# A graph-attention layer: the order of a group's work in the main loop is turned

## The chip, the cores and the metric

The kernel runs on one core of one Trainium2 chip. The metric is the device time of one execution in microseconds (us), the median of several runs. Five engines work side by side, each through its own queue in order: TensorE (PE), VectorE (DVE), ScalarE (ACT), GpSimd (POOL) and SyncE (SP). An instruction that waits holds up what is queued behind it on its engine.

## The reference

The layer has 12,500 nodes with 128 features and 212,500 edges, 12,500 of them self loops, sorted by target node (`dst`). There are 8 heads of 16 features.

```
Q, K, V = x @ WQ, x @ WK, x @ WV            # (N, 8, 16) each
Eh      = edge_attr @ WE                     # (E, 8, 16)
score   = exp(clip((K[src] * Q[dst] / sqrt(16) * Eh).sum(-1), -5, 5))
msg     = V[src] * score
wV, Z   = segment_sum(msg, dst), segment_sum(score, dst)
h       = x + wV / (Z + 1e-6)
h       = (h - mean) * rsqrt(var + 1e-5) * gamma + beta    # over the nodes
out     = layernorm(x + h)                   # over the features
```

## The kernel before

The edges are cut into 1,661 tiles of 128. A window of 64 nodes has its edges in four tiles, and a group is two windows, so eight tiles; there are 208 groups. `hx` keeps x in on-chip memory, features by nodes, and takes the sums in place.

The kernel has three stages. First the table: K and V of all nodes go to a table `kvd` in HBM, one row of 256 floats a node (up to about 105 us). Then the main loop, one group an iteration, to about 2,710 us. Then the two norms and the output.

The steps of a group g, with their lines and engines, are these. A line number is that of the kernel before.

- `gather` (L205, POOL): eight indirect transfers, each fetching 128 rows of K|V by source node into a slot. There are eight slots, and a ninth later. The loop hands queued transfers to POOL in two lots of four (`issue`); the first transfer of a lot waits (`pace`) for a step on DVE, the first lot for the message of the previous group (`SENT[g - 1]`), the second for the second half of the products (`PARTS[g][1]`).
- `load`, `load_rel`, `load_quad` (SP): edge features of two groups in one transfer of 1 MB, and the edges' places inside their window, on all partitions (`rb`, or `rbq` for four groups).
- `q_window` (L471, ACT) copies the x of the two windows to `xw`; `q_mm` (L502, PE) and `q_out` (L506, ACT) make Q of the 128 nodes in `qs`.
- `eh_mm` (L515, PE) and `eh_out` (L522, ACT): edge features times WE, into `wt`. `turned_onehot` (L492, DVE) compares places with node numbers, giving nodes by edges (`ot`). `qe_mm` (L529, PE) multiplies Q with it, so that each edge gets Q of its target.
- `both_halves` (L539, DVE) multiplies the two; `turn_back` (L547, PE) transposes the product, edge by edge, to `ps_t`.
- `products` (L562, DVE) multiply the gathered K by it, `scores` (L569, DVE) sum over each head, `clip_exp` clips on DVE (L578) and takes exp on ACT twice (L579, L580). `message` (L584, DVE) multiplies V by it and frees the slot.
- `onehot` (L482, L484, L485, DVE): edges by nodes (`oh`, two buffers). `gather_sum` (L599, L600, PE) multiplies it with the messages, which sums them by node in the PSUM bank `ps_a`; `sums_out` (L605, ACT) copies the sums out.
- `denom` (L609), `recip` (L612), `attn` (L616, all DVE) divide; `add_x` (L625, L626, PE) transposes the result and adds x; `x_out` (L630, ACT) writes it to `hx`. Batch-norm statistics (L633, DVE) follow where enough nodes are done.

No planner is at work: each engine takes its instructions in the order in which the loop's body (from L761) writes them, with waits added by the framework where a tile is read, or a buffer is used again. `sum_ps` (`ps_a`) holds three things side by side in one bank: the sums, Q's product and add_x's result. `ps_e`, `ps_q`, `ps_t` have two banks each. The loop before writes in iteration g, per engine:

- DVE: products(g), denom(g−2), scores(g), clip(g), recip(g−2), turned_onehot(g+2), both_halves(g+1), attn(g−2), message(g), onehot(g+1)
- PE: add_x(g−3), q_mm(g+2), gather_sum(g−1), eh_mm(g+2), turn_back(g+1), qe_mm(g+2)
- ACT: exps(g), x_out(g−3), q_out(g+2), sums_out(g−1), eh_out(g+2), q_window(g+3)

Of the kernel before, what the change touches and what calls it, by code (L numbers as in the profile page):

```python
# [8 lines left out]
F32 = mybir.dt.float32  # L9
BF16 = mybir.dt.bfloat16  # L10
U8 = mybir.dt.uint8
# [49 lines left out]
def gnn_kernel(  # L61
# [42 lines left out]
    kvd = dram.tile([N, 2 * P], F32, name="kvd")  # L104
    full = usizes.count(U) // 2
    assert usizes[:2 * full] == [U] * (2 * full)
    relT = dram.tile([2, full * U, P], BF16, name="relT")
    rel_end = dram.tile([T - full * G, P], BF16, name="rel_end")

# [99 lines left out]
    def issue(n=0):  # L211
        while len(queued) > n:
            f, *a = queued.pop(0)
            f(*a)
# [66 lines left out]
    def within(f, g):  # L281
        return f(g) if 0 <= g < NG else None
# [33 lines left out]
    def place(r):  # L316
        nc.vector.tensor_copy(vw(rel, r), vw(rel_i, r))
        nc.vector.tensor_tensor(vw(rel, r), vw(rel, r), bc(base_f, r), op=OP.subtract)
        end = ustarts[r[0]] + (r[1] - r[0]) * r[2]
        for t in range(ustarts[r[0]], end, P):  # L320
            n = min(P, end - t)
            ps, of = spare_ps, rel[:, t:t + n]
            apart = t + n <= full * G
            assert (t % G == n % G == 0) if apart else t >= full * G
            if apart:
                turned_of = wp.tile([P, P], F32, name="relby", bufs=1)
                nc.vector.tensor_copy(turned_of[:, :n].rearrange("p (h w j) -> p h w j", h=2, j=U),
                                      of.rearrange("p (w h j) -> p h w j", h=2, j=U))
                of = turned_of[:, :n]
            nc.tensor.transpose(ps[:n], of, ident)  # L330
            row = wp.tile([P, P], BF16, name="relrow", bufs=2)
            nc.vector.tensor_copy(row[:n], ps[:n])
            if apart:
                for h in (0, 1):
                    nc.scalar.dma_start(relT[h, t // 2:(t + n) // 2, :], row[h * n // 2:(h + 1) * n // 2])
            else:
                nc.scalar.dma_start(rel_end[t - full * G:t - full * G + n, :], row[:n])
# [4 lines left out]
        return bass.AP(tensor=relT.tensor, offset=relT.offset + (h * full + g) * U * P, ap=[[0, WN], [1, n * U * P]])  # L342

    def load_quad(q):
        t = late[0].tile([P, RQ, U * P], BF16, name="rbq", bufs=2)
        for h in (0, 1):
            nc.sync.dma_start(t[h * WN:(h + 1) * WN].rearrange("p a b -> p (a b)"), places(h, RQ * q, RQ))
        for k in range(RQ):
            RB[RQ * q + k] = t[:, k, :]
# [3 lines left out]
    def load_rel(g):  # L353
        if g // RQ in quads:
            return
        RB[g] = wp.tile([P, U * P], BF16, name="rb", bufs=2)
        for h in (0, 1):
            t, n = ustarts[2 * g + h] - full * G, usizes[2 * g + h]
            nc.sync.dma_start(RB[g][h * WN:(h + 1) * WN, :n * P], places(h, g, 1) if g < full else bass.AP(
                tensor=rel_end.tensor, offset=rel_end.offset + t * P, ap=[[0, WN], [1, n * P]]))  # L360
# [77 lines left out]
    def nt(g):  # L438
        return sizes[g]
# [15 lines left out]
    def project_main(g):  # L455
        half = [table_tile(2 * (g % 2) + a) for a in (0, 1)]
        KV[g] = lambda a, b, c, n=P: half[a // 4][:, a % 4:a % 4 + b - a, c:c + n]
        for a in (0, 4):
            project(g, a, lambda: turned().rearrange("p (a b) d -> p a (b d)", b=2), True)

    def q_window(g):
        if g not in BASE:
            n = 2 if g % 2 == 0 and g + 1 < NG else 1
            _, at = nc.values_load_multi_w_load_instructions(
                base_i[0:1, 2 * g:2 * (g + n)], engines=(ET.Activation,), min_val=0, max_val=N,
                skip_runtime_bounds_check_because="node ids")
            for k in range(n):
                BASE[g + k] = at[2 * k:2 * k + 2]
        XW[g] = wp.tile([P, P], F32, name="xw", bufs=6)
        for h in (0, 1):  # L470
            nc.scalar.activation(XW[g][:, h * WN:(h + 1) * WN], hx[:, ds(BASE[g][h], WN)], AF.Copy)  # L471

# [29 lines left out]
        return nc.tensor.matmul(PQ[g], XW[g], w_q, start=True, stop=True)  # L502

    def q_out(g):
        QS[g] = wp.tile([P, P], F32, name="qs", bufs=1)
        nc.scalar.activation(QS[g], PQ[g], AF.Copy, scale=0.25)  # L506

    EH = {}
# [22 lines left out]
    def ehqe(g):  # L531
        eh_mm(g)
        eh_out(g)
        qe_mm(g)
# [6 lines left out]
    def turn_back(g):  # L541

        PW[g] = []
        for h, (a, b) in enumerate(halves(g)):
            ps = turned()
            for j in range(b - a):
                nc.tensor.transpose(ps[:, j, :], WT[g][h][:, j * P:(j + 1) * P], ident)  # L547
            PW[g].append(ps)
# [15 lines left out]

    def scores(g, h=None):
        if not h:
            SS[g] = wp.tile([P, G, H], F32, name="s", bufs=1)
        for a, b in ranges(g, h):
            step = nc.vector.tensor_reduce(SS[g][:, a:b, :], KV[g](a, b, 0).rearrange("p t (h d) -> p t h d", d=DH),  # L569
                                           axis=AX.X, op=OP.add)  # L570
        PARTS.setdefault(g, []).append(step)

    def clip_exp(g, h=None):
        a, b = (0, nt(g)) if h is None else halves(g)[h]
        if not h:
            MSG[g] = wp.tile([P, G, W], F32, name="msg", bufs=2)
        s = SS[g][:, a:b, :]
        nc.vector.tensor_scalar(s, s, 5.0, -5.0, op0=OP.min, op1=OP.max)  # L578
        nc.scalar.activation(exp_ps(g)[:, a:b, :], s, AF.Exp)  # L579
        nc.scalar.activation(MSG[g][:, a:b, P:], s, AF.Exp)  # L580

    def message(g, h=None):
        for a, b in ranges(g, h):
# [91 lines left out]
    def both_halves(g):  # L675
        both(g, 0)
        both(g, 1)
# [4 lines left out]
             [(turned_onehot, 1)]]  # L682
    first_step = NQ - len(steps) - 5
    assert first_step > 3 and max(piece) < first_step + 14
    windows = {first_step + 2: (0, 1), first_step + 8: (2,)}
    for q in range(NQ):
        for w in windows.get(q, ()):
            q_window(w)
# [19 lines left out]
    load_kv()  # L708
    load(1)
    load_rel(2)  # L710
    ehqe(0)
    q_mm(1)
    q_out(1)
    both_halves(0)
    turn_back(0)
    ehqe(1)
    onehot(0)


    done = set()  # L720
# [31 lines left out]
    def within_checks(g):  # L752
        if g >= first_check and (g - first_check) % every == 0:
            check((g - first_check) // every)
# [6 lines left out]
    for g in range(NG - 2):  # L761
        if g % 2 == 0:
            load(g // 2 + 2)
        within(load_rel, g + 3)
        if (g + 6) % RQ == 0 and (g + 6) // RQ in quads:
            load_quad((g + 6) // RQ)
        within(products, g)
        within(denom, g - 2)
        within(scores, g)
        within(clip_exp, g)  # L770
        within(recip, g - 2)
        within(turned_onehot, g + 2)
        within(both_halves, g + 1)
        late_x = g + 1 < nxg and g + 1 not in SLOT
        if late_x:
            turn_x(g + 1, 0, True)
            turn_x(g + 1, 4, True)
        within(add_x, g - 3)
        within(q_mm, g + 2)
        if g < LATE + 4:  # L780
            issue()
        else:
            left = len(queued)
            for k, step in enumerate([SENT[g - 1], PARTS[g][1]]):
                if len(queued) == left - k * G // 2:
                    pace(step)
                issue(max(0, left - (k + 1) * G // 2))
        within(gather_sum, g - 1)
        if not late_x:
            within(eh_mm, g + 2)  # L790
        within(x_out, g - 3)
        within(q_out, g + 2)
        within(sums_out, g - 1)
        if late_x:
            project_main(g + 1)
            within(eh_mm, g + 2)
        within(eh_out, g + 2)
        within(q_window, g + 3)
        within(turn_back, g + 1)
        within(qe_mm, g + 2)  # L800
        within(attn, g - 2)
        within(message, g)
        within(onehot, g + 1)
        if g == 2:
            load_last()
        for r in runs[1:]:
            if g == max(4, r[0] // 2 - 12):
                place(r)
        within_checks(g)
        while free and todo and not pending:  # L810
            load_x()
        bn_parts(2 * g - 5, 2 * g - 3)
        if g == NG - 5:
            assert done >= set(range(NPRE))
            norm_first()
        if g == LATE - 1:
            tps.close()
            late.append(tps.enter_context(tc.tile_pool(name="late", bufs=1)))
        if g == LATE - 2:
            free.append(NSLOT)  # L820
            load_kv()
    last = NG - 1
    g = last - 1
    within_checks(g)
    within_checks(last)
    flag = [nc.values_load(bad_i[0:1, 0:1], min_val=0, max_val=1 << 20,
# [330 lines left out]
```

## Time and profile before

| what | value |
|---|---|
| median of 3 runs | 2780.78 us (2774.32 to 2784.37) |
| profiled execution | 2785.63 us, its span 2783.5 us |
| mean granted TensorE clock | 0.823 |
| busy share | PE 66%, DVE 56%, POOL 58%, ACT 21% |
| bytes moved | 386.26 MB, 139 GB/s |

The span runs from the first instruction to the last of the profiled execution. Busy is the time in which an engine executes; waits are idle time, put down to what ended last by the profile. A row of the groups reads: line, engine, operation, output and inputs, count, then busy us and mean ns of one, then the idle time just before and what ended most of it. A row of the timeline reads: start in us, duration in us, queue or engine, line, operation, count, and in brackets the idle time before it. The ends of matmuls are modelled.

### The profile page before, as it was taken

How to read it: one execution, taken by the hardware profiler on the slowest of the kernel's cores; microseconds unless marked ns; L12 is line 12 of the kernel's file. 1: busy time of each engine (PE TensorE's matmuls, PEld its weight loads, DVE VectorE, ACT ScalarE, POOL GpSimd, SP SyncE). 2: the span in 40 equal slices, each digit the busy share in tenths (PEclk: the TensorE clock that was granted, in tenths of full speed). 3: DMA queues.
4: the chain of work that ended last, by engine and by line, in shares of the span. 5: the costliest groups of instructions: out<-in, count | busy, mean ns of one | idle time of the engine just before them, and what ended most of it. 6: DMA issues, size and time to landing. Idle time of an engine off the chain costs nothing. (4 is left out here: it accounts for less than half of the span.)

```text
span 2783.5 us, 29268 instructions
## 1 busy us (share of the span) xinstructions
PE 1823.7 (66%) x8998; PEld 1169.4 (42%) x8998; DVE 1551.7 (56%) x3152; ACT 586.4 (21%) x2272; POOL 1602.5 (58%) x1697
## 2 busy tenths in 40 slices
PE   6667765766656756656566666666665666665688
PEld 5444443444333434433334334444343344333456
DVE  2335555555565646655555555655555565555578
ACT  1122121122111212221112121221211122211125
POOL 5644655655556656556565656556565665565524
PEclk8878878888888878887887878878787888788899
DMA  6634434444444444444444434444444444444443
GB/s 220 229 119 125 142 117 144 140 140 137 122 142 124 135 146 138 142 130 127 139 128 129 151 123 132 142 134 145 126 130 138 129 134 142 134 125 140 133 165 113
DMA packets 122250, 386.26 MB, mean 139 GB/s; under 512 B 34205, under 2 KB 42950, under 8 KB 108134
## 3 DMA queue, kind: packets, MB, share of 16 engines
q0 software_dynamic: 78704, 213.62, 26.2%
q1 hardware_dynamic: 40196, 169.36, 17.8%
q10 hardware_dynamic: 3186, 1.34, 0.2%
q8 instruction: 73, 1.20, 0.2%
q14 instruction: 91, 0.75, 0.1%
HBM read 364.56 MB, written 19.63 MB: 138 GB/s over the span
## 5 line engine op out<-in xcount | busy, mean ns | idle before, releaser
L205 POOL DMA_INDIRECT slot<-kvd,srcs x1597 | 1513.1, 947 | 1064.5 <-DVE rz L609 532.0
L529 PE MATMUL ps_q<-ot,qs 64*128 64x512 f32 x832 | 303.0, 812 | 722.1 <-ACT qs L506 709.0
L600 PE MATMUL ps_a<-msg,oh 128*128 128x136 f32 (+1 forms) x3322 | 557.2, 309 | 5.6 <-issue 4.7
L482 DVE TENSOR_TENSOR oh<-ps_m,rel_i 128x512 f32<-128x512 f32 x208 | 142.5, 685 | 698.6 <-remote 662.7
L600 PEld LDWEIGHTS ps_a<-msg,oh 128*128 128x128 f32 (+1 forms) x3322 | 457.9, 182 | 87.5 <-issue 64.0
L562 DVE TENSOR_TENSOR slot<-slot,ps_t 128x512 f32<-128x512 f32 x410 | 267.5, 679 | 336.7 <-remote 166.2
L515 PE MATMUL ps_e<-ea,w_e 128*128 128x512 f32 x832 | 399.4, 601 | 10.3 <-issue 7.0
L529 PEld LDWEIGHTS ps_q<-ot,qs 64*128 64x128 f32 x832 | 77.5, 228 | 768.6 <-ACT qs L506 728.1
L547 PE MATMUL ps_t<-ident,wt 128*128 128x128 f32 x1661 | 246.0, 284 | 138.2 <-DVE wt L539 71.8
L630 ACT ACTIVATE hx<-ps_a 128x64 f32 x408 | 90.6, 222 | 1070.4 <-remote 842.4
L547 PEld LDWEIGHTS ps_t<-ident,wt 128*128 128x128 f32 x1661 | 192.8, 143 | 289.2 <-DVE wt L539 140.4
L539 DVE TENSOR_TENSOR wt<-wt,ps_q 128x512 f32<-128x512 f32 x416 | 264.6, 673 | 20.6 <-remote 13.4
L522 ACT ACTIVATE wt<-ps_e 128x512 f32<-128x512 f32 x416 | 237.3, 612 | 61.8 <-PE ps_t L547 27.5
L569 DVE TENSOR_REDUCE s<-slot 128x64 f32<-128x1024 f32 (+1 forms) x208 | 249.9, 1202 | 0.2
L584 DVE TENSOR_TENSOR msg<-slot,ps_m 128x1024 f32<-128x1024 f32 (+2 forms) x209 | 247.5, 1186 | 0.4 <-ACT ps_m L579 0.3
L579 ACT ACTIVATE ps_m<-s 128x64 f32<-128x64 f32 (+1 forms) x209 | 47.5, 227 | 922.8 <-DVE s L578 554.5
L515 PEld LDWEIGHTS ps_e<-ea,w_e 128*128 128x128 f32 x832 | 144.9, 192 | 116.4 <-issue 111.2
L625 PEld LDWEIGHTS ps_a<-ident,at 128*128 128x128 f32 x408 | 74.6, 229 | 200.0 <-ACT xw L471 98.4
L625 PE MATMUL ps_a<-ident,at 128*128 128x128 f32 x408 | 120.0, 383 | 2.5 <-issue 1.1
L502 PE MATMUL ps_a<-w_q,xw 128*128 128x128 f32 x416 | 98.0, 324 | 8.2 <-ACT xw L471 4.6
L626 PE MATMUL ps_a<-xw,ident 128*128 128x128 f32 x408 | 95.5, 323 | 0.0
L471 ACT ACTIVATE xw<-hx 128x64 f32 x416 | 86.6, 271 | 12.1 <-DMA relT<-relrow 8.3
(174 smaller groups left out, 1406.3 us busy)
## 6 DMA issues: line engine op xcount, KB each, us to landing
ea<-eaT SPq DMA_DIRECT2D x103, 1024.0 KB
slot<-kvd,srcs POOLq DMA_INDIRECT x1597
rbq<-relT SPq DMA_DIRECT2D x94, 256.0 KB
kvd<-slot SPq DMA_DIRECT2D x12, 512.0 KB
kvd<-t SPq DMA_DIRECT2D x12, 512.0 KB
slot<-xT SPq DMA_DIRECT2D x6, 1024.0 KB
out<-o SPq DMA_DIRECT2D x23, 256.0 KB
hx<-xT SPq DMA_DIRECT2D x11, 512.0 KB
```

The source lines that it names most:

```text
L205: return nc.gpsimd.indirect_dma_start(out=out, out_offset=None, in_=table, in_offset=bass.IndirectOffsetOnAxis(ap=srcs[:, e:e + 1], axis=0))
L482: nc.vector.tensor_tensor(one, iota_ps[:, None, :].to_broadcast([P, n, P]), r[:, :n, None].to_broadcast([P, n, P]), op=OP.is_equal)
L515: nc.tensor.matmul(eh, w_e, EA[g][:, a:b, :].rearrange("p a b -> p (a b)"), start=True, stop=True)
L522: nc.scalar.activation(t[:, :(b - a) * P], EH[g][h], AF.Copy)
L529: nc.tensor.matmul(QE[g][h], QS[g][r], OT[g][r, :(b - a) * P], start=True, stop=True)
L539: nc.vector.tensor_tensor(t, t, QE[g][h], op=OP.mult)
L547: nc.tensor.transpose(ps[:, j, :], WT[g][h][:, j * P:(j + 1) * P], ident)
L562: step = nc.vector.tensor_tensor(kv, kv, PW[g][i][:, :b - a, :], op=OP.mult)
L569: step = nc.vector.tensor_reduce(SS[g][:, a:b, :], KV[g](a, b, 0).rearrange("p t (h d) -> p t h d", d=DH), axis=AX.X, op=OP.add)
L584: step = nc.vector.tensor_tensor(MSG[g][:, a:b, :P].rearrange("p t (h d) -> p t h d", d=DH), KV[g](a, b, P).rearrange("p t (h d) -> p t h ...
L600: nc.tensor.matmul(AGG[g][WN if j >= n else 0:], OH[g][j], MSG[g][:, j, :], start=(j == 0), stop=(j == n - 1))
L625: nc.tensor.matmul(ps, AT[g], ident, start=True, stop=False)
```

## The change

The order of the loop's body is turned. In iteration g the engines now have:

- DVE: message(g−1), both_halves(g+1), products(g), scores(g), clip(g), turned_onehot(g+3), onehot(g), denom, recip and attn of g−2
- PE: eh_mm(g+2), turn_back(g+1), qe_mm(g+2), add_x(g−3), q_mm(g+3), gather_sum(g−1)
- ACT: sums_out(g−2), eh_out(g+2), q_window(g+4), x_out(g−3), q_out(g+3), exps(g)

So the message of a group is written in the next iteration, its one-hot in the same iteration as its scores, and its sums are copied out one iteration after they are made; Q is made a group sooner. `clip_exp` is split, so that the clip and the exps can be placed apart. The edges' places are kept as bytes (U8) in place of BF16, which halves the tiles and the transfers of them; `xw` has 8 buffers for 6, `qs` and `s` 2 for 1. The gathers are handed out and paced as before: four after message(g−1), four after the second half of products(g). What comes ahead of the loop and behind it is fitted to the new order. `share` is the three divisions in one function, which was there before.

```diff
-    relT = dram.tile([2, full * U, P], BF16, name="relT")
-    rel_end = dram.tile([T - full * G, P], BF16, name="rel_end")
+    relT = dram.tile([2, full * U, P], U8, name="relT")
+    rel_end = dram.tile([T - full * G, P], U8, name="rel_end")
...
-                turned_of = wp.tile([P, P], F32, name="relby", bufs=1)
+                turned_of = wp.tile([P, 4, P], F32, name="xt", bufs=2)[:, 0, :]
...
-            row = wp.tile([P, P], BF16, name="relrow", bufs=2)
+            row = wp.tile([P, P], U8, name="relrow", bufs=2)
...
-        t = late[0].tile([P, RQ, U * P], BF16, name="rbq", bufs=2)
+        t = late[0].tile([P, RQ, U * P], U8, name="rbq", bufs=2)
...
-        RB[g] = wp.tile([P, U * P], BF16, name="rb", bufs=2)
+        RB[g] = wp.tile([P, U * P], U8, name="rb", bufs=2)
...
-        XW[g] = wp.tile([P, P], F32, name="xw", bufs=6)
+        XW[g] = wp.tile([P, P], F32, name="xw", bufs=8)
...
-        QS[g] = wp.tile([P, P], F32, name="qs", bufs=1)
+        QS[g] = wp.tile([P, P], F32, name="qs", bufs=2)
...
-            SS[g] = wp.tile([P, G, H], F32, name="s", bufs=1)
+            SS[g] = wp.tile([P, G, H], F32, name="s", bufs=2)
...
-    def clip_exp(g, h=None):
+    def clip(g, h=None):
+        a, b = (0, nt(g)) if h is None else halves(g)[h]
+        s = SS[g][:, a:b, :]
+        nc.vector.tensor_scalar(s, s, 5.0, -5.0, op0=OP.min, op1=OP.max)
+
+    def exps(g, h=None):
         a, b = (0, nt(g)) if h is None else halves(g)[h]
         if not h:
             MSG[g] = wp.tile([P, G, W], F32, name="msg", bufs=2)
         s = SS[g][:, a:b, :]
-        nc.vector.tensor_scalar(s, s, 5.0, -5.0, op0=OP.min, op1=OP.max)
         nc.scalar.activation(exp_ps(g)[:, a:b, :], s, AF.Exp)
         nc.scalar.activation(MSG[g][:, a:b, P:], s, AF.Exp)
+
+    def clip_exp(g, h=None):
+        clip(g, h)
+        exps(g, h)
...
     load_kv()
     load(1)
     load_rel(2)
+    load_rel(3)
     ehqe(0)
     q_mm(1)
     q_out(1)
     both_halves(0)
+    turned_onehot(2)
     turn_back(0)
     ehqe(1)
-    onehot(0)
+    q_mm(2)
+    q_out(2)
 
 
     done = set()
@@ -761,22 +772,24 @@
     for g in range(NG - 2):
         if g % 2 == 0:
             load(g // 2 + 2)
-        within(load_rel, g + 3)
+        within(load_rel, g + 4)
         if (g + 6) % RQ == 0 and (g + 6) // RQ in quads:
             load_quad((g + 6) // RQ)
+        within(sums_out, g - 2)
+        within(message, g - 1)
+        within(both_halves, g + 1)
+        within(eh_mm, g + 2)
+        within(eh_out, g + 2)
         within(products, g)
-        within(denom, g - 2)
-        within(scores, g)
-        within(clip_exp, g)
-        within(recip, g - 2)
-        within(turned_onehot, g + 2)
-        within(both_halves, g + 1)
         late_x = g + 1 < nxg and g + 1 not in SLOT
         if late_x:
             turn_x(g + 1, 0, True)
             turn_x(g + 1, 4, True)
-        within(add_x, g - 3)
-        within(q_mm, g + 2)
+            project_main(g + 1)
+        within(turn_back, g + 1)
+        within(qe_mm, g + 2)
+        within(scores, g)
+        within(clip, g)
         if g < LATE + 4:
             issue()
         else:
@@ -785,22 +798,16 @@
                 if len(queued) == left - k * G // 2:
                     pace(step)
                 issue(max(0, left - (k + 1) * G // 2))
+        within(add_x, g - 3)
+        within(q_mm, g + 3)
+        within(q_window, g + 4)
+        within(x_out, g - 3)
+        within(q_out, g + 3)
+        within(exps, g)
         within(gather_sum, g - 1)
-        if not late_x:
-            within(eh_mm, g + 2)
-        within(x_out, g - 3)
-        within(q_out, g + 2)
-        within(sums_out, g - 1)
-        if late_x:
-            project_main(g + 1)
-            within(eh_mm, g + 2)
-        within(eh_out, g + 2)
-        within(q_window, g + 3)
-        within(turn_back, g + 1)
-        within(qe_mm, g + 2)
-        within(attn, g - 2)
-        within(message, g)
-        within(onehot, g + 1)
+        within(turned_onehot, g + 3)
+        within(onehot, g)
+        within(share, g - 2)
         if g == 2:
             load_last()
         for r in runs[1:]:
@@ -821,6 +828,9 @@
             load_kv()
     last = NG - 1
     g = last - 1
+    sums_out(g - 2)
+    message(g - 1)
+    onehot(g)
     within_checks(g)
     within_checks(last)
     flag = [nc.values_load(bad_i[0:1, 0:1], min_val=0, max_val=1 << 20,
```

More of the change, by code (lines that the diff above doesn't have):

```diff
@@ L684, in gnn_kernel @@
     assert first_step > 3 and max(piece) < first_step + 14
-    windows = {first_step + 2: (0, 1), first_step + 8: (2,)}
+    windows = {first_step + 2: (0, 1), first_step + 8: (2, 3)}
     for q in range(NQ):
```

## The prediction

> **What bounds the kernel now.** I read the page first, for the totals.
>
> ```profile
> span 2783.5 us, 29268 instructions
> ...
> PE 1823.7 (66%) x8998; PEld 1169.4 (42%) x8998; DVE 1551.7 (56%) x3152; ACT 586.4 (21%) x2272; POOL 1602.5 (58%) x1697
> L205 POOL DMA_INDIRECT slot<-kvd,srcs x1597 | 1513.1, 947 | 1064.5 <-DVE rz L609 532.0
> ```
>
> No engine is near full. The pace of the loop is that of the clip (L578), once a group:
>
> ```profile
> L578 DVE TENSOR_SCALAR s<-s x177: 194/194/453, 432.5 to 2678.6; 128x64 f32<-128x64 f32 x177
> ```
>
> That is (2678.6 − 432.5)/176 = 12.76 us a group. Eight gathers of 947 ns, started 1.25 us apart (below), fill only 10.0 of it. The view of waits says what stands still:
>
> ```profile
> DVE oh L482 <- remote: 662.7, 60, 11.8
> ACT hx L630 <- remote: 842.4, 65, 14.5
> PE ps_q L529 <- ACT qs L506: 709.0, 61, 13.0
> POOL slot L205 <- DVE rz L609: 532.0, 124, 9.7
> ```
>
> Some 60 times VectorE, ScalarE and TensorE stop together for over 11 us: 177 groups / 60, every third group. "Remote" means that no instruction ends near the wait's end. The timeline of one case (start, duration, engine, line):
>
> ```profile
> 1541.49 0.95 POOL L205 DMA_INDIRECT slot<-kvd,srcs  x1 [2.72 <-DVE rz L609]
> ...
> 1543.85 1.25 PE L547 MATMUL ps_t<-ident,wt 128*128 128x128 f32 x8 [1.90 <-issue]
> ...
> 1545.04 1.13 PE L529 MATMUL ps_q<-ot,qs 64*128 64x512 f32 x4
> ...
> 1546.64 0.39 PE L502 MATMUL ps_a<-w_q,xw 128*128 128x128 f32 x2
> ...
> 1546.87 1.93 PE L600 MATMUL ps_a<-msg,oh 128*128 128x136 f32 x14
> ...
> 1549.05 0.50 PE L600 MATMUL ps_a<-msg,oh 128*128 128x136 f32 x2
> ...
> 1560.27 0.95 POOL L205 DMA_INDIRECT slot<-kvd,srcs  x1 [0.30 <-issue]
> 1564.21 0.69 DVE L482 TENSOR_TENSOR oh<-ps_m,rel_i 128x512 f32<-128x512 f32 x1 [11.44 <-remote]
> 1564.27 0.48 ACT L630 ACTIVATE hx<-ps_a 128x64 f32 x2 [14.14 <-remote]
> ...
> 1564.65 0.27 ACT L506 ACTIVATE qs<-ps_a 128x128 f32<-128x128 f32 x1
> 1564.81 0.29 ACT L605 ACTIVATE os<-ps_a 128x136 f32<-128x136 f32 x1
> ...
> 1564.97 2.08 PE L529 MATMUL ps_q<-ot,qs 64*128 64x512 f32 x4 [12.84 <-ACT qs L506]
> ...
> 1565.41 1.27 DVE L562 TENSOR_TENSOR slot<-slot,ps_t 128x512 f32<-128x512 f32 x2
> ...
> 1566.96 0.94 POOL L205 DMA_INDIRECT slot<-kvd,srcs  x1 [5.74 <-DVE rz L609]
> 1566.98 0.79 PE L625 MATMUL ps_a<-ident,at 128*128 128x128 f32 x2
> ```
>
> What L482 and L630 wait for is the last matmul of gather_sum (L600). Its record ends at 1549.55, 8.1 us after an unbroken run of 16 gathers began; it is acted on at 1564.2, 3.0 us after that run's last gather (1560.27 + 0.95 = 1561.22). The next run, of 8, shows the other side:
>
> ```profile
> 1572.05 0.50 PE L600 MATMUL ps_a<-msg,oh 128*128 128x136 f32 x2
> ...
> 1572.58 0.69 DVE L482 TENSOR_TENSOR oh<-ps_m,rel_i 128x512 f32<-128x512 f32 x1 [1.33 <-issue]
> ...
> 1574.10 1.04 PE L547 MATMUL ps_t<-ident,wt 128*128 128x128 f32 x8
> ...
> 1574.30 0.60 ACT L522 ACTIVATE wt<-ps_e 128x512 f32<-128x512 f32 x1 [0.26 <-PE ps_e L515]
> ...
> 1575.71 0.95 POOL L205 DMA_INDIRECT slot<-kvd,srcs  x1 [0.30 <-issue]
> ...
> 1576.91 0.69 DVE L562 TENSOR_TENSOR slot<-slot,ps_t 128x512 f32<-128x512 f32 x1 [3.04 <-PE ps_a L625]
> ...
> 1579.32 0.95 POOL L205 DMA_INDIRECT slot<-kvd,srcs  x1 [2.66 <-DVE rz L609]
> ```
>
> This run starts at 1566.96. Sums ending at 1572.55 (age 5.6 us) are seen at once, and L515's end is at 1574.30 (age 7.3). The transposes end at 1575.14 (age 8.2), and L562, which reads them, starts only at 1576.91, 0.25 us after the run. So I read: **a TensorE result is seen by other engines at once up to about 7.3 us into a run of gathers; from 8.1 us on it is held until the run ends, 3.0 us more after 16.** Why, the trace does not say.
>
> One cycle, from 1541.49 to 1579.32, is 37.8 us for 24 gathers or three groups. Written out: 24 × 1.25 = 30.0 of gathers and 5.74 + 2.66, less twice the 0.30 between any two gathers, 7.8 of extra pause. Per group it is 10.0 plus (pauses)/3. What the change is worth is read from two things: how many groups are served per hold, and how long the chain from its release to the next gather is.
>
> **The change part by part.** The counts of instructions on each engine stay; the order turns.
>
> Durations of a group's work on DVE and of the first exps on ACT:
>
> ```profile
> L584 DVE TENSOR_TENSOR msg<-slot,ps_m 128x1024 f32<-128x1024 f32 x201 | 242.7, 1208 | 0.0
> L539 DVE TENSOR_TENSOR wt<-wt,ps_q 128x512 f32<-128x512 f32 x414 | 263.8, 674 | 20.6 <-remote 13.4 <-PE ps_q L529 4.0 <-PE ps_e L515 2.1
> L569 DVE TENSOR_REDUCE s<-slot 128x64 f32<-128x1024 f32 x202 | 246.4, 1220 | 0.2
> L492 DVE TENSOR_SCALAR ot<-rbq,wiota 128x512 f32<-128x512 bf16 x188 | 87.2, 464 | 0.0
> L579 ACT ACTIVATE ps_m<-s 128x64 f32<-128x64 f32 x207 | 47.1, 228 | 922.8 <-DVE s L578 554.5 <-DVE s L569 184.3 <-issue 147.5
> ```
>
> *Byte-wide positions.* The loads of positions on SP halve (256 to 128 KB each); no wait above names them, so 0. L492 then reads u8. Bounds: no change at 0.46 us, a gain of half of it, or the 0.63 us of half an L562 pair (1.27) if it runs as those do: −0.2 to +0.2 us a group. DVE stands still for 11 us in every third group and, in my layout below, for 1.6 us in each; that covers it, so 0. If the cover were gone, 0.2 × 176 = 35 us. The extra buffers (xw, qs, s) only take waits away: 0. Positions asked for a group sooner go past one load of edges on SP's queue; they are wanted a group sooner as well, 0.
>
> TensorE's next matmuls after the stop, and two stretches of the table by windows, the stop and what follows it:
>
> ```profile
> 1568.65 3.15 PE L600 MATMUL ps_a<-msg,oh 128*128 128x136 f32 x13
> ```
>
> ```profile
> 1552.80:1564.20 11.40, 0.00 (x0) 0.00 (x0) 0.00 (x0) 0.00 (x0) 6.59 (x7) 0.57 0.32 93
> 1564.20:1570.00 5.80, 5.03 (x17) 3.27 (x18) 5.72 (x13) 2.46 (x10) 2.43 (x3) 0.50 0.64 213
> ```
>
> The granted clock (third figure from the right) falls in the stop and is 0.50 in the 5.8 us after it.
>
> *The loop.* I lay one iteration by hand, t = 0 at message(g−1), POOL idle.
> - DVE: message to 1.2; it releases four gathers, so a run starts at 1.5. Both halves of L539 to 2.5, products (1.27) to 3.7, which releases the other four. Scores and clip to about 5.1, one-hots turned to 5.5.
> - PE: the second four transposes start when products end, 0.6; then from L529's start to L502's end as above (1545.04 to 1547.03), 2.0. So q_mm ends at 6.3, age 4.8: seen.
> - ACT: x_out, q_out and then exps, a new place: 0.38 + 0.16 + about 0.3 for L579 makes 7.15. Now onehot(g) stands behind exps(g), which stands behind x_out and q_out, which wait for q_mm: a serial chain that before had a group of slack. DVE idles 1.6.
> - DVE: onehot 1.2 (1564.21 to 1565.41), share about 0.5: the next message at 8.8.
> - PE: gather_sum(g−1) waits for q_out (6.9) and takes 2.7 (1546.87 to 1549.55): it ends at 9.6, **age 8.1**.
>
> Message(g) at 8.8 releases four more gathers at 10.0, before the first eight end at 11.5, and products(g+1) the last four: a run of 16, to 1.5 + 20.0 = 21.5. With age 8.1 the sums are held like those at 1549.55. Then ACT stops at sums_out(g−1); behind it in its queue are eh_out, x_out, q_out and exps(g+1). PE stops at add_x(g−2), whose bank sums_out must have read; behind it are q_mm and gather_sum(g). DVE stops at onehot(g+1), which waits for the exps; behind it are share and message(g+1), and POOL's pacing waits for that message, with nothing of POOL's own in between. At 24.5 the hold ends. Next is late, in series: sums_out 0.3; add_x and q_mm at the low clock 1.7 (from 1566.98 to 1568.65, where gather_sum follows); x_out, q_out, exps 0.85; onehot 1.2; share 0.5: message at 29.1. **Two groups take 29.1 us, 14.55 each**, 1.79 more than 12.76; over 176 groups +315 us.
>
> If instead the sums at age 8.1 still pass (the edge lies between 7.3 and 8.1), x_out is what is held, one iteration on, with q_mm at age 13. Then 0.85 + 1.2 + 0.5 and 0.2 follow the release, message comes at 27.2, and two groups take 13.6 each: +0.84 × 176 = +148. Ends: 2785.6 + 148 = 2934 and 2785.6 + 315 = 3101. The profiled run lies 4.9 us over the median 2780.8; 5 us off gives 2929 and 3096. My age of 8.1 is that of the held row, so I take the upper part: **3060**. The first 25 groups and the tail I leave as they are.
>
> **The rivals.**
> - *One group per hold (slower still).* If TensorE still is at the low clock at tb and qe (L529 takes 2.08 instead of 1.13), q_mm ends up to 2.3 us later, age 7.1, at the edge. Beyond it exps and onehot are held until the run of 8 is over at 11.5, plus 0.3 to 1.7 (1576.66 to 1576.91, and the next half), plus 2.6 to the message: 14.4 to 15.8, so 2781 + 1.6 × 176 to 2781 + 3.0 × 176, 3070 to 3315. The clock decides it: tb comes 8 us after a release here, the rows show 0.50 for at least 5.8 us. The Trainium skill, "TensorE: Matmul & The Clock Gate", Part 1 on the HAM clock gate, says that the array is back at full clock after about 3.4 us of sustained work. By that rule the transposes would be fast in every iteration and this rival would have hardly a chance; the rows show the halved clock for longer than the page has it, so some is left.
> - *The other side: no hold binds.* If what is held depends not on the run's age but on something that the new order avoids (sums now lie last on PE, with a message that is a group old), DVE's chain of 8.8 is shorter than POOL's 10.0. POOL then runs through: −2.7 × 176 = −485, 2295; at 10.6 with small pauses 2400. For it: the sums' record is the one that is late in every long stop. Against: the transposes at 1575.14 are late too, after 8.2 us. It decides if sums_out follows gather_sum at an age over 8.
> - *Partly so: three or four groups per hold.* With a release chain of 4 to 6 us, three give (30.0 + 3.0 + 5)/3 = 12.7, no change; four give (40.0 + 8)/4 = 12.0, 2645. DVE would have to be a group further ahead than the queue on ACT allows.
> - *The change does nothing:* the same three groups per hold with the old chain. The trace has nothing for it.
>
> **How the numbers follow.** Two per hold 0.50; one 0.13; no hold 0.20; four 0.11; three 0.06, of which half within 0.3%, which is about what a measurement can tell from no change. Faster 0.20 + 0.11 + 0.02 = 0.33, same 0.03, slower 0.64. Leaving out most of the no-hold cases (0.16) and little at the top, the range is 2600 to 3260; that of the likeliest case alone 2900 to 3150.
>
> **What would show it.** Right: L482 waits about 90 times for 8 to 11 us, now behind ACT's L583 (the exps); sums_out's activation (L605 before, L613 after) takes over ACT's long waits; POOL runs of 16 with pauses near 9 us; L578 every 13.6 to 14.6 us. Wrong: gathers run on past 16 with no pause, or L613 starts right after sums that end over 8 us into a run. Then the age was not the cause. L492 far over 0.68 us would also upset the sum.

## The result and the profile after

The changed kernel takes 3004.7 us (median of 4 runs, 3000.1 to 3028.4), 1.082 times the kernel before (interval 1.077 to 1.088) on the chip of this comparison. The prediction said 3060, within 2600 to 3260. The profiled execution has a span of 2998.9 us against 2783.5.

One thing comes first, since everything below depends on it. All kernels of one comparison run on one chip, but the comparisons went to several chips, and the kernel before does not take the same time on them: 2772 us on chip 4, 2750 on chip 1, but 2144 on chip 10 and 2145 on chip 14. The chip of this first comparison (2781), whose number is not on record, behaves like chips 4 and 1. On chip 14 the change costs 1.0% (interval 0.9 to 1.2), not 8.2%. The experiments show what differs.

The page of the kernel after, groups with their busy time, mean ns, and the idle time before them:

```profile
span 2998.9 us, 29250 instructions
...
L205 POOL DMA_INDIRECT slot<-kvd,srcs x1597 | 1531.8, 959 | 1247.2 <-DVE msg L592 745.7
...
L482 DVE TENSOR_TENSOR oh<-ps_m,rel_i 128x512 f32<-128x512 f32 x208 | 143.8, 691 | 1248.1 <-ACT ps_m L583 885.3
...
L613 ACT ACTIVATE os<-ps_a 128x136 f32<-128x136 f32 x208 | 59.1, 284 | 1447.4 <-remote 702.2
...
L492 DVE TENSOR_SCALAR ot<-rbq,wiota 128x512 f32<-128x512 uint8 x188 | 90.3, 480 | 0.0
```

Busy times hardly move; the idle time in front of L482 grows from 699 to 1248 us, and that of POOL from 1065 to 1247. L482 now waits for the exps (L583), and most of ACT's long "remote" waits have gone from x_out to sums_out (L613). The clip's line, once a group, in the window from 450 us on, gives the pace:

```profile
L576 DVE TENSOR_SCALAR s<-s x176: 195/195/319, 452.3 to 2876.6; 128x64 f32<-128x64 f32 x176
```

(2876.6 − 452.3)/175 = 13.85 us a group, after 12.76. The line of before, in the prediction, holds one group more. Its last 175 groups run from 451.0 to 2678.6, 2227.6 us, where these take 2424.3. So the loop makes 197 of the 215 us by which the span grew, and 17 come behind it. The timeline of two cycles and of the run behind them (start, duration):

```profile
1512.20 1.21 DVE L592 TENSOR_TENSOR msg<-slot,ps_m 128x1024 f32<-128x1024 f32 x1
...
1513.69 0.95 POOL L205 DMA_INDIRECT slot<-kvd,srcs  x1 [8.28 <-DVE msg L592]
...
1518.78 0.39 PE L502 MATMUL ps_a<-w_q,xw 128*128 128x128 f32 x2
...
1519.48 0.48 ACT L638 ACTIVATE hx<-ps_a 128x64 f32 x2 [2.19 <-PE ps_a L502]
...
1520.18 2.03 PE L608 MATMUL ps_a<-msg,oh 128*128 128x136 f32 x14 [1.01 <-ACT hx L638]
...
1522.25 1.21 DVE L592 TENSOR_TENSOR msg<-slot,ps_m 128x1024 f32<-128x1024 f32 x1
1522.46 0.50 PE L608 MATMUL ps_a<-msg,oh 128*128 128x136 f32 x2
...
1532.61 0.94 POOL L205 DMA_INDIRECT slot<-kvd,srcs  x1 [0.30 <-issue]
1536.45 0.28 ACT L613 ACTIVATE os<-ps_a 128x136 f32<-128x136 f32 x1 [16.03 <-remote]
...
1539.23 3.73 PE L608 MATMUL ps_a<-msg,oh 128*128 128x136 f32 x14 [0.80 <-ACT qs L506]
...
1539.33 0.69 DVE L482 TENSOR_TENSOR oh<-ps_m,rel_i 128x512 f32<-128x512 f32 x1 [11.60 <-ACT ps_m L583]
...
1541.30 1.21 DVE L592 TENSOR_TENSOR msg<-slot,ps_m 128x1024 f32<-128x1024 f32 x1
...
1542.79 0.94 POOL L205 DMA_INDIRECT slot<-kvd,srcs  x1 [9.23 <-DVE msg L592]
...
1546.06 1.04 PE L547 MATMUL ps_t<-ident,wt 128*128 128x128 f32 x8
...
1552.72 1.21 DVE L592 TENSOR_TENSOR msg<-slot,ps_m 128x1024 f32<-128x1024 f32 x1
...
1554.21 0.95 POOL L205 DMA_INDIRECT slot<-kvd,srcs  x1 [1.60 <-DVE msg L592]
...
1559.09 0.39 PE L502 MATMUL ps_a<-w_q,xw 128*128 128x128 f32 x2
...
1565.10 0.48 ACT L638 ACTIVATE hx<-ps_a 128x64 f32 x2 [7.30 <-remote]
...
1567.87 1.21 DVE L592 TENSOR_TENSOR msg<-slot,ps_m 128x1024 f32<-128x1024 f32 x1
...
1569.35 0.95 POOL L205 DMA_INDIRECT slot<-kvd,srcs  x1 [5.32 <-DVE msg L592]
```

The first cycle is the one that the prediction laid by hand. A run of 16 gathers lasts from 1513.69 to 1533.55. Sums that end at 1522.96 are acted on at 1536.45, 2.9 us after the run, and the next run begins at 1542.79: 29.1 us for two groups. The second is another kind. The message at 1552.72 comes after the eight gathers have ended (1552.6), and POOL pauses for 1.60 us. The run of 8 behind this pause is held again: q_mm (L502) ends at 1559.48, 5.3 us into the run, x_out (L638) acts on it only at 1565.10, 1.1 us after the run, and the next message comes at 1567.87. Counted from POOL's rows between 450 and 2,890 us, with a pause over 0.5 us as the end of a run, there are 39 runs of 16 with a mean pause of 9.08 us behind them, and 91 runs of 8 with one of 3.43. The second mean is of two kinds: 39 of the 91 pauses are under 1.9 us, as at 1552.6, and 36 are over 3.9, as at 1564.0.

### The profile page after: what moved, and what is told of

Same layout as the page of the kernel before. It is cut to its first block, busy times and chain, and to the rows that moved or that the text cites. A ratio compares the mean times of both kernels' runs of the same rounds, so it can differ in the third digit from the quotient of the medians.

```text
span 2998.9 us, 29250 instructions
## 1 busy us (share of the span) xinstructions
PE 1971.9 (66%) x8998; PEld 1277.5 (43%) x8998; DVE 1594.0 (53%) x3152; ACT 611.4 (20%) x2272; POOL 1621.4 (54%) x1697
## 5 line engine op out<-in xcount | busy, mean ns | idle before, releaser
L205 POOL DMA_INDIRECT slot<-kvd,srcs x1597 | 1531.8, 959 | 1247.2 <-DVE msg L592 745.7
L608 PE MATMUL ps_a<-msg,oh 128*128 128x136 f32 (+1 forms) x3322 | 729.6, 375 | 513.5 <-ACT qs L506 371.0
L608 PEld LDWEIGHTS ps_a<-msg,oh 128*128 128x128 f32 (+1 forms) x3322 | 571.0, 217 | 666.1 <-ACT qs L506 399.5
L482 DVE TENSOR_TENSOR oh<-ps_m,rel_i 128x512 f32<-128x512 f32 x208 | 143.8, 691 | 1248.1 <-ACT ps_m L583 885.3
L515 PE MATMUL ps_e<-ea,w_e 128*128 128x512 f32 x832 | 413.7, 621 | 2.0 <-ACT t L252 1.4
L613 ACT ACTIVATE os<-ps_a 128x136 f32<-128x136 f32 x208 | 59.1, 284 | 1447.4 <-remote 702.2
L547 PE MATMUL ps_t<-ident,wt 128*128 128x128 f32 x1661 | 236.6, 277 | 94.1 <-DVE slot L562 63.4
L529 PE MATMUL ps_q<-ot,qs 64*128 64x512 f32 x832 | 236.8, 646 | 0.0
L638 ACT ACTIVATE hx<-ps_a 128x64 f32 x408 | 91.8, 225 | 613.2 <-remote 279.6
L515 PEld LDWEIGHTS ps_e<-ea,w_e 128*128 128x128 f32 x832 | 159.7, 213 | 114.2 <-issue 111.7
L607 PE MATMUL ps_a<-os,carry 64*1 64x136 f32 x414 | 98.3, 325 | 0.0
L502 PE MATMUL ps_a<-w_q,xw 128*128 128x128 f32 x416 | 93.4, 312 | 0.0
L492 DVE TENSOR_SCALAR ot<-rbq,wiota 128x512 f32<-128x512 uint8 x188 | 90.3, 480 | 0.0
```

The costliest lines, as they stand in the source:

```text
L205: return nc.gpsimd.indirect_dma_start(out=out, out_offset=None, in_=table, in_offset=bass.IndirectOffsetOnAxis(ap=srcs[:, e:e + 1], axis=0))
L482: nc.vector.tensor_tensor(one, iota_ps[:, None, :].to_broadcast([P, n, P]), r[:, :n, None].to_broadcast([P, n, P]), op=OP.is_equal)
L515: nc.tensor.matmul(eh, w_e, EA[g][:, a:b, :].rearrange("p a b -> p (a b)"), start=True, stop=True)
L529: nc.tensor.matmul(QE[g][h], QS[g][r], OT[g][r, :(b - a) * P], start=True, stop=True)
L608: nc.tensor.matmul(AGG[g][WN if j >= n else 0:], OH[g][j], MSG[g][:, j, :], start=(j == 0), stop=(j == n - 1))
```

## The experiments

Three theories stood against each other. Theory 1: the age of an unbroken run of gathers holds TensorE's results. Theory 2: the new order is slow by its own serial chain. Theory 3: the bytes in flight hold the results. Where a kernel fills half of the tiles by a direct transfer, its edges get the K and V of other nodes, and no arithmetic is left out.

**Half the gathers (chip 4, before 2772.5 us).** Each group gathers four tiles, and SP fills the other four.

```diff
-            for j in range(sizes[g]):
+            m = G // 2 if steady[0] else sizes[g]
+            if m < sizes[g]:
+                r = 512 * (g % 24)
+                nc.sync.dma_start(KV[g](m, sizes[g], 0, 2 * P), kvd[r:r + P * (sizes[g] - m), :]...)
+            for j in range(min(m, sizes[g])):
...
-                if len(queued) == left - k * G // 2:
+                if len(queued) == left - k * G // 4:
                     pace(step)
-                issue(max(0, left - (k + 1) * G // 2))
+                issue(max(0, left - (k + 1) * G // 4))
```

> The changed kernel, but in the main loop only four of a group's eight tiles are gathered; the other four are filled by one direct transfer of SP with 512 consecutive rows of the table, the same bytes, so these edges get other nodes' K and V. Theory 1 (age): a TensorE result is held once gathers have run unbroken for some 7 us. A group's gathers then take 5.0 us, runs stay short of that, nothing is held, and a group takes the chain of 8.8 to 9.5 us: 1950 to 2200 us in all. Theory 2 (chain): the new order costs its time by itself, with or without gathers: 2850 to 3000. Theory 3 (data): results are held by the bytes in flight, which are the same: 2850 to 3000.

> The same halving in the kernel before. Theory 1: no long stops, a group takes DVE's own 7.0 to 7.8 us: 1680 to 1900 us. Theories 2 and 3: its long stops stay in every third group: 2600 to 2780. By theory 1 it stays ahead of the halved changed kernel, since the new chain (8.8) is longer than DVE's work (7.0).

The changed kernel so halved took 2181.9 us (ratio 0.787, interval 0.783 to 0.790), the kernel before 1696.9 (0.612, 0.610 to 0.614). The line of the clip in both, halved before first:

```profile
L583 DVE TENSOR_SCALAR s<-s x168: 195/195/324, 403.9 to 1597.4; 128x64 f32<-128x64 f32 x168
```

```profile
L581 DVE TENSOR_SCALAR s<-s x166: 195/195/320, 409.4 to 1995.3; 128x64 f32<-128x64 f32 x166
```

These are 7.15 and 9.61 us a group. The bytes are the same, so theory 3 falls, and the long stops are gone, as theory 1 said. Both times lie in the ranges that it gave. Theory 2 is partly right: with nothing held the new chain costs 9.6 us where the old order costs 7.15. But eight gathers take 10.0, so this alone does not make a kernel with all its gathers slower.

**exps ahead of x_out (chip 4).**

```diff
         within(clip, g)
+        within(exps, g)
...
-        within(exps, g)
```

> The changed kernel with exps(g) written right after clip(g), so that on ACT it stands ahead of x_out and q_out and onehot no longer waits for q_mm. Theory 1: sums stay held and exps of the next group stays behind sums_out, so the long stops stay, but add_x, q_mm, x_out and q_out leave the chain from a release to the next message (4.6 us becomes 2.4): about 1.1 us a group in runs of 16, 2790 to 2900 us in all. Theory 2: the chain of 8.8 becomes 7.2 and no long stop is left: 2700 or less.

It took 3006.7 us (1.084, 1.078 to 1.090): no gain, so this expectation failed. The waits of this kernel (total us, times, longest):

```profile
DVE oh L482 <- ACT ps_m L583: 941.6, 148, 13.1
ACT os L613 <- remote: 813.7, 67, 17.2
...
ACT hx L638 <- remote: 451.6, 92, 7.2
...
DVE at L624 <- PE ps_a L502: 93.9, 72, 1.9
DVE at L624 <- remote: 63.6, 27, 3.5
```

ACT's long waits have grown (702 to 814 for L613, 280 to 452 for L638), and there is a new one: the division (L624) has one buffer and waits for add_x, a TensorE result too. The shorter chain was given back in waits of the same kind. POOL's rows, counted as above, now have 54 runs of 16 with a mean pause of 8.20 us and 64 of 8 with one of 3.40: the long hold is 0.9 us cheaper, but more groups go through it. How much the buffer costs is open: the kernel with two (exps_at) ran on a chip without holds.

> exps_early with a second buffer for the divided sums (at), since there attn waits for add_x, which is held. Theory 1: this wait goes and DVE gets further before it stops at the next onehot; sums stay held. 2800 to 2950 us. If it stays at 3000, another held TensorE result takes the place of this one.

On chip 10 it took 2151.9 us beside 2143.6 (1.004, 1.002 to 1.006), which says nothing about the held case.

**A pause after every eight gathers.** The first gather of a group also waits until an earlier one has landed: the last (flush_after, and flush_before at the products' second half), or the last but one (flush7).

```diff
-                    pace(step)
+                    pace(step, sent[-1] if k == 0 else None)   # flush7: sent[-2]; flush_before: k == 1
```

The rest of the edit, not shown, keeps the gathers in a list `sent` and lets `pace` wait for one of them.

> The changed kernel, but the first gather of each group also waits until the last one of the group before has landed, so POOL pauses some 1.9 us after every eight gathers. Theory 1: no run is longer than 8, what is held comes free in every group, and a group takes 10.0 + 1.6 to 2.5 us: 2560 to 2750 us in all. Theory 2, and any reading in which the pauses are only lost time: 3000 us or more.

flush_after on chip 4 took 2716.7 us, 0.979 of the kernel before (0.977 to 0.982), and 288 us less than the changed kernel took in the first comparison (it was not run on chip 4 itself; exps_early took 3006.7 there). POOL does the same work and waits for its own landing:

```profile
POOL slot L207 <- DMA slot<-kvd,srcs: 427.6, 154, 5.7
```

```profile
L582 DVE TENSOR_SCALAR s<-s x180: 195/195/446, 409.0 to 2590.5; 128x64 f32<-128x64 f32 x180
```

That is 12.19 us a group, within the 10.0 + 1.6 to 2.5 expected. Waiting longer made the kernel faster, which only theory 1 says. On a chip without holds it was not run.

> The kernel before, but the gather that waits for the products' second half waits too until the gather ahead of it has landed. Theory 1: no run is longer than 8, the long stops of every third group go, and a group takes what the runs of 8 took, 12.4, or POOL's 10.0 + 2.3: 2650 to 2760 us. If pauses are only lost time: 2850 or more.

> As flush_after, but the first gather of a group waits for the landing of the last but one, so the pause falls from 2.5 to some 1.3 us. If a pause of this length lets held results through, a group takes 11.1 to 11.6 us: 2480 to 2600 us. If not (a pause of 0.87 us did not), runs of 16 and more in effect, with long stops: 2800 to 3050.

These two ran on chip 10, where the kernel before takes 2143.6 us: 2763.9 (1.290, 1.284 to 1.295) and 2403.7 (1.121, 1.118 to 1.125). Nothing is held there (below), so these two times decide nothing about holds: the pause is only lost time. In flush_before POOL pauses 3.6 us on average behind eight gathers, longer than the 2.3 expected, and the products wait for gathers to land (1017 us in all). flush7 ran twice more.

> flush7_after once more. Where results are held: 2480 to 2600 us if a pause of 1.3 us in every eight gathers lets them through, 2800 to 3050 if not. Where nothing is held, 2400 us again, the pause being only lost time.

> flush7_after once more, wanted on the same kind of chip: 2480 to 2600 us if a pause of 1.3 us after every eight gathers lets held results through, 2800 to 3050 if not. Where nothing is held 2400 again.

On chip 14 it took 2405.5 us (1.122, 1.119 to 1.124). On chip 1 (before 2750.2) it took 2859.2 (1.039, 1.036 to 1.042), in the range for a pause that does not let results through. Only 80 of its 181 pauses are under 1.5 us, since POOL waits for the message as well. The timeline of that run:

```profile
1510.00 1.13 PE L535 MATMUL ps_q<-ot,qs 64*128 64x512 f32 x4
...
1510.40 0.95 POOL L207 DMA_INDIRECT slot<-kvd,srcs  x1 [1.29 <-DMA slot<-kvd,srcs]
...
1512.26 0.28 ACT L619 ACTIVATE os<-ps_a 128x136 f32<-128x136 f32 x1 [8.41 <-PE ps_q L535]
...
1513.15 0.39 PE L508 MATMUL ps_a<-w_q,xw 128*128 128x128 f32 x2
...
1522.31 0.48 ACT L644 ACTIVATE hx<-ps_a 128x64 f32 x2 [7.73 <-remote]
```

The sums that sums_out (L619) waited for at 1510 came free 1.9 us into the next run. q_mm, which ended 3.1 us into that run (1513.54), was then held to 1522.31, far below the age of 7 us: the short pause had not set the age back. So a result can also come free while a run goes on, which the prediction's reading did not have.

**POOL busy with something else.** The halved changed kernel, with two iotas after each gather.

```diff
+            spin = late[0].tile([P, 512], I32, name="spin", bufs=1)
+            for _ in range(2):
+                nc.gpsimd.iota(spin, pattern=[[1, 512]], base=0, channel_multiplier=0)
```

> The halved changed kernel (four of eight tiles gathered, the rest by a direct transfer of other rows), and after each gather of the late loop two iotas on POOL that nobody reads, some 1.1 us, so that POOL is again busy for about 10 us a group without a gap, with half the gathers. Theory 1 in its narrow form (what holds is the back-to-back issue of gathers): nothing is held, a group takes POOL's 9.5 to 10.5 us, 2250 to 2450 us in all. In its wide form (any unbroken work of POOL holds): long stops come back and the time is 2800 to 3050.

> busy_after once more, wanted on a chip where the kernel before takes some 2775 us. There, narrow theory 1 (back-to-back gathers hold): 2140 to 2450 us. Wide form (any unbroken work of POOL): 2800 to 3050. Where the kernel before takes 2144 us: 2147 again.

On chip 10 it took 2147.2 us (1.002, 1.000 to 1.004), which settles nothing there. On chip 1, where results are held, it took 2187.0 (0.795, 0.791 to 0.798), within the second range, below the first one (2250 to 2450), and close to the 2181.9 without the iotas on chip 4. Its POOL rows on chip 1:

```profile
1499.71 1.20 POOL L210 IOTA spin<- 128x512 int32 x2
1501.32 0.95 POOL L205 DMA_INDIRECT slot<-kvd,srcs  x1 [0.41 <-DVE msg L602]
1502.28 1.19 POOL L210 IOTA spin<- 128x512 int32 x2
1503.62 0.95 POOL L205 DMA_INDIRECT slot<-kvd,srcs  x1 [0.15 <-issue]
```

POOL works almost without a gap and there are no long stops. So gathers issued one behind another, 1.25 us apart, go with holds; 2.3 us apart, with other work of POOL between, they don't. Whether their rate counts, or how many of them are under way at once, these runs do not separate.

**The change once more, on whatever chip.**

> The changed kernel as it is, beside the kernel before. On a chip where the kernel before takes some 2775 us (long runs of gathers hold TensorE's results), 1.08 of it, 3000 us. On a chip where it takes some 2144 us, as in the last four comparisons, nothing is held and POOL's 10.0 us a group is the bound for both orders, since the new chain of 8.8 us is shorter: ratio 0.995 to 1.01, 2135 to 2165 us. If the new order cost time by its own chain (theory 2), 1.05 or more there too.

On chip 14 the changed kernel took 2167.3 us, the kernel before 2145.4: 1.010 (1.009 to 1.012), 2 us over the range. Its timeline, and its waits of POOL:

```profile
1510.95 0.94 POOL L205 DMA_INDIRECT slot<-kvd,srcs  x1 [0.31 <-issue]
1511.48 0.50 PE L608 MATMUL ps_a<-msg,oh 128*128 128x136 f32 x2
1512.02 0.28 ACT L613 ACTIVATE os<-ps_a 128x136 f32<-128x136 f32 x1 [4.06 <-PE ps_a L608]
1512.20 0.95 POOL L205 DMA_INDIRECT slot<-kvd,srcs  x1 [0.30 <-issue]
```

```profile
POOL slot L205 <- issue: 456.6, 1498, 0.3
```

From 430 us on 1,344 gathers follow each other without a break, 10.07 us a group, and sums that end at 1511.98 are copied out at 1512.02, in the middle of a run hundreds of gathers old. So on this chip nothing is held, and the gathers bound the loop. Where the 1.0% arises was not shown, since no profile of the kernel before was taken there. exps_at, on chip 10, is 15 us shorter; between 90 and 470 us POOL pauses 26.3 us in the changed kernel and 11.7 in exps_at, which points at the first dozen groups.

**When the results become visible.** An engine that waits for a result waits for the semaphore update of the engine that made it, and the packed traces hold the times at which these updates were recorded. I compare each recorded update in the main loop with the last end of a matmul before it that sends one, so that the delay is a lower bound.

| kernel, chip | TensorE's updates on record | over 0.5 us late | latest, us |
|---|---|---|---|
| before, first comparison | 1249 | 549 | 12.4 |
| after, first comparison | 1307 | 541 | 9.9 |
| exps_early, chip 4 | 1224 | 638 | 11.0 |
| flush7_third, chip 1 | 1299 | 546 | 10.7 |
| flush_after, chip 4 | 1310 | 410 | 4.5 |
| half_before, chip 4 | 1161 | 79 | 0.8 |
| half_after, chip 4 | 1055 | 38 | 1.2 |
| busy_again, chip 1 | 1221 | 0 | under 0.15 |
| after_again, chip 14 | 1382 | 0 | under 0.15 |
| flush_before, chip 10 | 1350 | 0 | under 0.15 |

VectorE's and ScalarE's updates are not late in any of these. In the first cycle above, six updates of TensorE, for work that ended from 1522.96 to 1527.69, are recorded from 1536.43 to 1536.69, while those of VectorE at 1523.48, 1524.67, 1525.87 and 1527.35 come on time. So it is TensorE's update that is late, and it is late with gathers 1.25 us apart and on some chips only. One thing more sets these chips apart: their traces lack a part of the updates, those of VectorE and ScalarE and of landed DMAs too. Of DMA landings, the changed kernel's trace has 8,163 records in the first comparison and 32,071 on chip 14. Every run on record comes with a recorded span and clock, so whether the recording has a part in the holds was not tested.

## Why the prediction was right, and where it was not

- *Holding by runs of gathers* was the ground of the forecast, and the runs bear it out: halved gathers and a pause of 2.5 us came out as it says, gathers spaced out by iotas are not held, and TensorE's updates are on record as late. That it depends on the chip was not in the prediction at all. The range was right for a chip that holds; on chip 14 the same change gives 2167 us.
- *Two groups per hold, 29.1 us* is a cycle that the trace has, to a tenth (1513.69 to 1542.79), but only 39 times, for 78 of the 169 groups counted in runs of 8 and 16. L482's waits behind L583 came 111 times with a mean of 8.0 us (foretold: about 90 times, 8 to 11), the pauses behind runs of 16 are 9.08 us (near 9), and L613 took over ACT's long waits (702 us in 48).
- *The step that was mis-sized* is the iteration of 8.8 us. It takes 10.05 in the first cycle (1512.20 to 1522.25) and 11.4 in the second (1541.30 to 1552.72), and 9.6 where nothing is held. I had left out that TensorE, after a release, has gather_sum at the low clock (fourteen of its matmuls take 3.73 us from 1539.23, and 2.03 from 1520.18) and the edge product (L515) ahead of the transposes. The first eight gathers take 10.0, so the message comes just before their end or just after it. In 91 of 130 runs it came after: 8 × 1.25 + 3.43 − 0.30, 13.1 us a group; in some of them because q_mm was held (next point). With the 14.4 of the runs of 16 that makes 13.7, near the 13.85 measured and below the 14.35 behind 3060. So the number came out near for a mixture of cycles, not for the single one that I laid.
- *One group per hold* was priced as the slower rival, at 14.4 to 15.8 us: q_mm held until a run of 8 is over. It happened, at 15.1 us in the run from 1554.21 to 1569.35, but next to groups that get by without a hold (11.4 us, 1542.79 to 1554.21), so that the two together cost less than a cycle of 16. The clock was not the reason: the transposes at 1546.06 are at full clock, 1.04 us for eight. The granted clock, by windows of 1 us, is 0.50 up to 1544, 0.69 to 1545 and 1.00 behind that, some 5 us after gather_sum began at 1539.23. The rule of the Trainium skill ("TensorE: Matmul & The Clock Gate", Part 1), full clock after about 3.4 us of sustained work, is right that these transposes are fast, but the trace takes longer to get there.
- *The age counted from the last gap* was too simple, and this is what brings the rival on. Of q_mm's that end 4 to 7 us into a run, 28 of 33 are acted on over 4 us late where the pause before the run was under 1.9 us, and none of 93 where it was longer. So a result can be held from 4.8 us of a run on, not only from 7.3 to 8.1, when the pause before was short. A pause of 0.88 us sets nothing back either:

```profile
730.35 0.50 PE L608 MATMUL ps_a<-msg,oh 128*128 128x136 f32 x2
...
731.62 0.95 POOL L205 DMA_INDIRECT slot<-kvd,srcs  x1 [0.88 <-issue]
...
740.19 0.28 ACT L613 ACTIVATE os<-ps_a 128x136 f32<-128x136 f32 x1 [11.89 <-remote]
```

  Sums that end at 730.85 are seen neither in the pause nor in the first 7 us of the next run. They come free at 740.19, while that run still goes on. With pauses of 2.5 us and more (flush_after) holds remain, but short ones: no update is recorded over 4.5 us late.
- *No hold binds* does happen, on chips 10 and 14, but not because of the order. The kernel before is very likely free of holds there as well: its time is 2144, and flush_before, which is that kernel with more waits, has no late update. On chip 14 the change takes 2167 us, not the 2295 to 2400 priced, because the first groups go faster too, which I had left as they are: the 34th clip comes at 430 us there, and at 565 in the kernel before.
- *Positions as bytes* cost nothing seen: L492 takes 480 ns instead of 464.

## What to carry to other kernels

When several engines stop together and the wait ends with no instruction near it, look at what else ran without a break and test it by thinning it out; busy shares will not show it. An order that puts more steps in series behind a release pays them at every release, even when each engine has time to spare; shortening that chain alone (exps ahead of x_out) gained nothing here. Before believing a few per cent, run the kernel before on another chip: here the same two programs are 8% apart on one and 1% on another.

## What was not expected of the hardware

The same program takes 2750 to 2781 us on some chips and 2144 on others. On the first, TensorE's results stay unseen for up to 15 us (1549.55 to 1564.2 in the prediction) while gathers are issued 1.25 us apart; in the traces from the others they don't. A pause of under 1.9 us between runs of gathers does not end this in the trace of the changed kernel. On the first kind, adding a wait of 2.5 us per group to POOL saved 288 us against the changed kernel of the first comparison, and replacing half of the gathers by direct transfers of the same bytes took the kernel before from 2772 to 1697 us. Why chips differ, and what path the held results share with the gathers, no run here shows.
